# Values split into two float32r parts, tokens kept by super tile, and later weights turned earlier in a four-layer graph kernel

## The chip, the cores and the metric

The kernel runs on one core of one Trainium2 chip. A core has five engines that run their own instruction streams and wait for each other through semaphores: TensorE (PE; its weight loads are listed as PEld), VectorE (DVE), ScalarE (ACT), GpSimd (POOL) and SyncE (SP), which here does nothing but issue transfers. Transfers run on 16 DMA engines and are issued from SP, ACT or POOL. The metric is the device time of one execution in microseconds (us), as the median of several runs.

## The reference, cut to what matters

There are N = 3327 tokens x of 128 features, a dense matrix adj (3327 x 3327), and four layers, each followed by a residual and a layer norm. Layer 0 is an attention over 128 "slots" with 8 values each; the other three are graph layers with adj.

```python
# layer 0: n, d = x.shape; h = 8
q = (x @ Wq.T).reshape(d, n, h)
k = (x @ Wk.T).reshape(d, n, h)
v = (x @ Wv.T).reshape(d, n, h)
a = einsum('dnh,dmh->dnm', q, k) * scale + adj + adj
out = einsum('dnm,dmh->dnh', softmax(a, axis=2), v).reshape(n, h * d) @ Wo.T
x = layernorm(x + out)
# layers 1 to 3: adj (normalized) @ x, times small weights, residual, layernorm
```

The reshape is plain: the 3327 x 1024 result of a projection is read in memory order as 128 rows of 3327 x 8. So slot row d begins at token 3327 d / 128, mostly not at a multiple of anything convenient, and the q, k and v of one slot row come from about 26 neighbouring tokens.

## The kernel before, in words

The kernel has three stages. In the profiled execution the prologue lasts until the first exponential at 339 us, the attention until the last exponential starts at 10,018 us, and the three graph layers until the end at 10,791 us. The change touches the prologue alone (lines 243 to 408).

**The prologue** goes through the tokens in NU = 7 super tiles of 512 tokens (the last has 255). `load_by_h` loads and transposes Wq, Wk and Wv. For every super tile x is loaded (`xr`, line 264), transposed on TensorE (`xtr`, line 271) and copied to SBUF in two orders: `xT` by VectorE for q and k, and `xN` by ScalarE for the values. Before, all seven super tiles have room in one `xT` and one `xN`.

The main loop then takes each super tile u in turn.

- `split` (line 339) makes q, and then k: `products` (two matmuls of 512 columns a slot of 128 tokens) into a PSUM buffer `pp` of which there are two; ScalarE writes the rounded high part `hi` as float32r, VectorE the remainder `lo`, and VectorE reduces `hi` to a maximum (`top_q` or `top_k`, line 348). POOL issues the stores of `hi` and `lo` to DRAM (`q_s`, `k_s`), 2 MB each.
- `values_projected` (line 303) makes the values transposed, one matmul a head h into a PSUM buffer `pv`, copied by ScalarE and VectorE in turn to `vp`.
- `values_turned(d)` (line 312) brings the values of two slot rows d and d + 1 into the layout that the attention reads: a matmul with a shifted identity (a 128 column window of `turn`, which is zeros, identity, zeros) moves tokens to their partition and transposes at once. A slot row's window can lie across the end of the partitions (`wrap`) and two super tiles, so one call has some four matmuls, mostly of 8 x 26 = 208 columns, into a PSUM buffer `vtr`. VectorE and ScalarE copy these in turn to `vo`, and after every eight calls ScalarE issues four stores `v_img<-vo` (line 336).
- For u = 1 to 4 a row tile `ar` of adj is loaded by SP (line 88 in `load_rows`) and its maximum `tops` taken by VectorE (line 368). `ar` and `vo` share the tag "wide", of which there are two buffers. `store_tops` (line 217) writes the maxima in pieces of 4 bytes to `lead_s`.

`xtr`, `pv` and `vtr` share three PSUM buffers (tag "ps"); `w_ps`, for the transposes of weights, has one.

After the loop, in the order of the text, the weights of later layers (w1, w3, wo) are loaded, transposed and stored to DRAM, and a global maximum is reduced over partitions (`topall`, line 391) into a flag.

**What sets the order.** In the prologue a scheduler orders each engine's instructions by its own estimate of times; an engine then runs them strictly in that order. It moves work across the text: in the program as built, the transposes of x stand several super tiles ahead of their use, and those of w1, w3 and wo lie between matmuls from super tile 1 on. The attention has its order written out by hand (`manual_schedule`, line 663 on) and is the same before and after. Its SBUF pools take the room of the prologue's, so its first load (`e_in`, line 439) waits until all of the prologue's transfers are done.

Of the kernel before, what the change touches and what calls it, by code (L numbers as in the profile page):

```python
# [10 lines left out]
F32 = mybir.dt.float32  # L11
F32R = mybir.dt.float32r
I32 = mybir.dt.int32
AF = mybir.ActivationFunctionType
# [5 lines left out]
P = 128  # L20
# [30 lines left out]
def kernel(ctx: ExitStack, tc: tile.TileContext, x, adj, wq, wk, wv, wo,  # L51
# [193 lines left out]
    with tc.tile_pool(name="pw", bufs=1) as pw, tc.tile_pool(name="pa", bufs=2) as pa, \  # L245
# [9 lines left out]
        xT = pw.tile([P, NU, 4, P], F32, name="xT")  # L255
        xN = pw.tile([P, NU * SUPER], F32, name="xN")
        wqT = load_by_h(pw, ppw, wq, "wqT")
        for u in range(NU):
            base, R, full, rest = spread(u)
            xr = pa.tile([P, 4, D], F32, name="xr")  # L260
# [11 lines left out]
            nc.vector.tensor_copy(xT[:, u, 0:R, :], ps[:, 0:R, :])  # L272
            nc.scalar.copy(xN[:, base:base + R * P].rearrange("c (p r) -> c r p", r=R), ps[:, 0:R, :])
            if u == 0:
                wkT = load_by_h(pw, ppw, wk, "wkT")
                wvT = load_by_h(pw, ppw, wv, "wvT")
# [9 lines left out]
        def products(u, r, w):  # L286
            pp = pps.tile([P, HD], F32, tag="pp", name="pp")
            for c in range(0, HD, 512):
                nc.tensor.matmul(pp[:, c:c + 512], lhsT=xT[:, u, r, :], rhs=w[:, c:c + 512], start=True, stop=True)
            return pp.rearrange("p (h j) -> p h j", h=H)  # L290
# [7 lines left out]
        turn = pw.tile([P, 3 * P], F32, name="turn")  # L298
        nc.gpsimd.memset(turn, 0.0)
        nc.gpsimd.tensor_copy(turn[:, P:2 * P], ident)  # L300
        vp, vo = {}, {}

        def values_projected(u):
            n = spread(u)[1] * P
            vp[u] = pa.tile([P, H, SUPER], F32, name="vp")
            for h in range(H):
                ps = pps.tile([P, SUPER], F32, tag="ps", bufs=3, name="pv")
                nc.tensor.matmul(ps[:, 0:n], lhsT=wvT[:, h * D:(h + 1) * D], rhs=xN[:, u * SUPER:u * SUPER + n],
                                 start=True, stop=True)
                copy(h, vp[u][:, h, 0:n], ps[:, 0:n])  # L310

        def values_turned(d):
# [5 lines left out]
            for k in range(2):  # L318
                q, r = (d + k) * N // D, (d + k) * N % D
                for wrap in range(2 if r else 1):  # L320
                    at = q + wrap
                    while at < q + wrap + T:
# [4 lines left out]
                        nc.tensor.matmul(ps[:, k, :, s:s + n], lhsT=turn[:, first:first + P],  # L327
                                         rhs=vp[u][:, :, at - u * SUPER:at - u * SUPER + n],
                                         start=(k == 0 and wrap == 0 and s == 0), stop=True,
                                         skip_group_check=True)  # L330
# [26 lines left out]
        for u in range(NU):  # L357
            split(u, wqT, q_s, top_q, SCALE / 2)
# [6 lines left out]
            if 1 <= u <= 4:  # L365
                ar = pa.tile([P, NP], F32, tag="wide", name="ar")
                load_rows(nc.sync, ar[:, 0:N], adj, u - 1)
                nc.vector.tensor_reduce(tops[:, u - 1:u], ar[:, 0:N], AX.X, ALU.max)
            if u == 4:
                store_tops(pw, 0, tops, P)  # L370
        assert d == D

        w1T = load_transposed(pw, ppw, w1, "w1T")
        nc.gpsimd.dma_start(out=w1T_s, in_=w1T.rearrange("p a b -> p (a b)"))
        w3T = load_transposed(pw, ppw, w3, "w3T")
        nc.gpsimd.dma_start(out=w3T_s, in_=w3T.rearrange("p a b -> p (a b)"))

        wo_raw = pw.tile([P, HD], F32, tag="w_raw", name="wo_raw")
        nc.sync.dma_start(out=wo_raw, in_=wo)
        woT = pw.tile([P, HD], F32, name="woT")  # L380
        for h in range(H):
            ps = ppw.tile([P, P], F32, tag="w_ps", name="w_ps")
            nc.tensor.transpose(ps, wo_raw.rearrange("p (j h) -> p h j", h=H)[:, h, :], ident)
            copy(h, woT[:, h * D:(h + 1) * D], ps)
        nc.gpsimd.dma_start(out=woT_s, in_=woT)
# [863 lines left out]
```

## Time and profile before

| | |
|---|---|
| median of 3 runs | 10783.05 us (10782.16 to 10786.95) |
| profiled execution | 10792.99 us, span 10791.2 us |
| TensorE, VectorE, ScalarE busy over the span | 10545.2, 8700.0, 9680.6 us |
| last value store's copies end, first load of the attention, first exponential | 310.0, 317.1, 339.1 us |
| moved by DMA from 0 to 360 us | 86.51 MB |

Three kinds of answers are used below. A row of a group of instructions has: line, engine, operation, tile written <- tiles read, shapes, count | total busy us, mean ns of one | idle time of the engine just before, and what ended it. A row of windows has: stretch, length, then busy time (and count) of PE, PEld, DVE, ACT and POOL, granted TensorE clock, DMA share and GB/s. A row of the timeline has: start, length, engine, line, operation, count, and in brackets the idle time ahead of it with what ended it. A float32 matmul shows as two records; a float32r matmul or a transpose as one. [...]records in a stream overlap, and their spacing is what they cost.

### The profile page before, as it was taken

The numbers are of one execution on the slowest core, as the hardware profiler recorded it, in microseconds if no ns is written. First come the engines' busy times: TensorE is split into PE (matmuls) and PEld (weight loads), VectorE is DVE, ScalarE is ACT, GpSimd is POOL, SyncE is SP. The second block draws the span as 40 slices with busy tenths as digits, with TensorE's granted clock in tenths as the row PEclk, the third lists the DMA queues.
The fourth block names the chain that finished last, engine by engine and source line by source line (L and its number), as shares of the span: only waits on it lengthen the run. The fifth ranks groups of instructions, "written<-read, shape, count | busy, mean of one in ns | idle before, by whom it ended". The sixth has DMA issues, their size and how long they took to land. (4 is left out here: it accounts for less than half of the span.)

```text
span 10791.2 us, 203132 instructions
## 1 busy us (share of the span) xinstructions
PE 10545.2 (98%) x76941; PEld 4103.4 (38%) x76941; DVE 8700.0 (81%) x9695; ACT 9680.6 (90%) x10559; POOL 1852.8 (17%) x2742
## 2 busy tenths in 40 slices
PE   8899999999999999999999999999999999999999
PEld 5333333333333333333333333333333333333779
DVE  6688998889988899888899788998889877788412
ACT  3799999999999999999999999999999999999400
POOL 0111122111221122211122111121112100001200
PEclk9899999999999999999999999999999999999999
DMA  7888888888888888888888788888888888888676
GB/s 251 156 129 124 131 139 136 128 126 129 136 140 125 125 132 135 137 125 128 129 139 137 116 123 122 125 132 129 129 128 126 124 120 118 115 114 121 214 281 246
DMA packets 995965, 1516.25 MB, mean 141 GB/s; under 512 B 203368, under 2 KB 813474, under 8 KB 981164
## 3 DMA queue, kind: packets, MB, share of 16 engines
q1 hardware_dynamic: 897750, 1371.76, 78.7%
q0 software_dynamic: 79616, 116.88, 4.9%
q8 instruction: 624, 10.22, 0.5%
q10 hardware_dynamic: 17620, 14.49, 0.4%
q14 instruction: 355, 2.90, 0.1%
HBM read 1371.86 MB, written 130.35 MB: 139 GB/s over the span
## 5 line engine op out<-in xcount | busy, mean ns | idle before, releaser
L618 ACT ACTIVATE e<-sc 128x952 f32<-128x952 f32 (+1 forms) x10080 | 9458.5, 1090 | 247.6 <-PE sc L610 216.5
L636 PE MATMUL o<-e,v_pad 128*32 128x476 f32 (+1 forms) x46592 | 5621.3, 573 | 38.2 <-DVE acc L649 25.5
L610 PE MATMUL sc<-qt,kt 64*128 64x476 f32 x23296 | 4470.2, 438 | 113.8 <-ACT e L618 63.6
L610 PEld LDWEIGHTS sc<-qt,kt 64*128 64x128 f32 x23296 | 2166.0, 184 | 4415.6 <-ACT e L618 3840.0
L580 DVE SCALAR_TENSOR_TENSOR e<-e,ey 128x952 f32<-128x952 f32 x2016 | 2319.7, 1151 | 66.4
L515 POOL COPY v_pad<-vs 128x192 f32<-128x192 f32 (+1 forms) x896 | 606.7, 702 | 7666.8 <-DMA vs<-v_img 5875.9
L636 PEld LDWEIGHTS o<-e,v_pad 128*32 128x32 f32 (+1 forms) x46592 | 1045.1, 108 | 1967.2 <-issue 1931.9
L574 DVE TENSOR_SCALAR ey<-sc 128x952 int32<-128x952 f32 x672 | 772.1, 1149 | 624.6 <-PE sc L610 615.1
L501 DVE CAST qt<-qt 64x1904 fp32r<-64x1904 f32 x896 | 1041.5, 1162 | 30.4
L499 DVE TENSOR_SCALAR qt<-qt 32x1428 fp32r<-32x1428 f32 x896 | 809.0, 903 | 140.4 <-DMA qt<-q_s 109.5
L234 POOL DMA_DIRECT2D adjT_s<-at x1352 | 853.5, 638 | 232.6 <-DMA adjT_s<-at 168.2
L580 DVE SCALAR_TENSOR_TENSOR e<-ey 128x952 f32<-128x952 f32 x672 | 773.5, 1151 | 23.3
L580 DVE SCALAR_TENSOR_TENSOR e<-e,et 128x952 f32<-128x952 f32 x672 | 774.1, 1152 | 20.7
L1085 PE MATMUL bank<-y,eT 128*128 128x128 f32 (+1 forms) x4056 | 473.9, 276 | 0.4 <-DVE h L1207 0.4
L1085 PEld LDWEIGHTS bank<-y,eT 128*128 128x128 f32 (+1 forms) x4056 | 465.3, 192 | 5.7 <-DVE h L1207 0.6
L577 DVE TENSOR_SCALAR ey<-ey 128x952 int32<-128x952 int32 x672 | 447.1, 665 | 23.3
L575 DVE TENSOR_SCALAR et<-ey 128x952 int32<-128x952 int32 x672 | 443.1, 659 | 22.5
L500 DVE TENSOR_SCALAR qt<-qt 32x476 fp32r<-32x476 f32 x896 | 385.7, 430 | 6.2 <-DMA qt<-lead_s 3.2
L649 DVE TENSOR_TENSOR acc<-o,acc 128x476 f32<-128x476 f32 x231 | 150.4, 651 | 248.8 <-PE o L636 247.6
L1045 ACT ACTIVATE rstd<-mv,eps 128x1 f32<-128x1 f32 x104 | 30.4, 293 | 265.2 <-DVE mv L1043 265.2
L656 POOL DMA_DIRECT2D o_s<-acc x308 | 238.7, 779 | 30.0 <-DVE acc L649 20.2
L647 DVE COPY acc<-o 128x476 f32<-128x476 f32 x77 | 50.1, 650 | 136.4 <-PE o L636 135.8
(151 smaller groups left out, 2357.8 us busy)
## 6 DMA issues: line engine op xcount, KB each, us to landing
kt<-k_s SPq DMA_DIRECT2D x5320, 96.0 KB
kt<-k_s SPq DMA_DIRECT2D x1764, 128.0 KB
eT<-adjT_s SPq DMA_DIRECT2D x78, 1664.0 KB
qt<-q_s SPq DMA_DIRECT2D x896, 119.0 KB
qt<-q_s SPq DMA_DIRECT2D x1792, 59.5 KB
vs<-v_img SPq DMA_DIRECT2D x224, 224.0 KB
adjT_s<-at POOLq DMA_DIRECT2D x1352, 32.0 KB, 6.3
vs<-v_img SPq DMA_DIRECT2D x224, 192.0 KB
```

Of the source, the lines that this page charges most:

```text
L234: nc.gpsimd.dma_start(out=flat_ap(adjT_s, (t * P + 32 * q) * NP + c * PIECE, [[NP, 32], [P, ns], [1, P]]), in_=at[32 * i:32 * i + 32].rear ...
L499: return [(0.9, None, lambda: nc.vector.tensor_scalar(qt[32:64, 1:], qf[0:32, 0:GROUP - 1], -1.0, None, ALU.mult)), (0.4, None, lambda: nc ...
L501: (1.2, None, lambda: nc.vector.tensor_copy(qt[64:128], qf[0:64]))]
L515: nc.gpsimd.tensor_copy(vp[:, 32:32 + nt * GROUP * 32].rearrange("p (x c) -> p x c", c=32)[:, :, 0:H], vs.rearrange("p (x c) -> p x c", c=H))
L574: nc.vector.tensor_scalar(yi, x, -58 * math.log(2.0), 2 ** 24 / math.log(2.0), ALU.max, ALU.mult)
L575: vec.append((0.7, of, lambda: nc.vector.tensor_scalar(ti, yi, UPPER, EXPONENT, ALU.bitwise_and, ALU.bitwise_xor)))
L577: vec.append((0.7, of, lambda: nc.vector.tensor_scalar(yi, yi, LOWER, QUARTER, ALU.bitwise_and, ALU.bitwise_or)))
L580: vec.append((1.2, of, lambda i=i, a=a: nc.vector.scalar_tensor_tensor(e, e if i else y, a, t if i == len(POLY) - 1 else y, ALU.add, ALU.m ...
L610: nc.tensor.matmul(s[:, i, 0:CW], lhsT=kt[64 * rg:64 * rg + 64, k, pos * P:(pos + 1) * P], rhs=qt[64 * rg:64 * rg + 64, k, :], start=False ...
L618: nc.scalar.activation(e[:, 0:n, :], s[:, 0:n, 0:CW], AF.Exp, scale=2.0)
L636: nc.tensor.matmul(o[32 * j:32 * j + 32, 0:CW], lhsT=values[b, g][:m, c:c + 32], rhs=es[b, g * GROUP + j, r][:m, :], start=(r == 0 and u = ...
L1085: nc.tensor.matmul(ps[:n, 0:D], lhsT=e[:m, s, :n], rhs=y[:m, s, col:col + D], start=(s == 0), stop=(s == T - 1))
```

## The change

There are three parts.

1. The projected values are kept as two float32r parts: `hi`, written by ScalarE from PSUM with rounding, and `lo`, the remainder, by VectorE from PSUM and `hi`. `values_turned` multiplies each part with a shifted identity in float32r and sums both in PSUM. Where a window has an odd number of tokens, both parts go through a float32 matmul with a float32 identity (`moves`) instead.
2. `xT` and `xN` are tiles of one super tile in a pool of two, and `tokens_turned(u)` is called at the start of super tile u instead of for all u ahead of the loop. This makes room for the second part of `vp`.
3. The weights w1, w3 and wo are loaded, transposed and stored within the loop, after super tile 2, instead of after the loop.

```diff
--- before.py
+++ after.py
@@ -252,11 +252,13 @@
             R = (n + P - 1) // P
             return base, R, n // R, n % R
 
-        xT = pw.tile([P, NU, 4, P], F32, name="xT")
-        xN = pw.tile([P, NU * SUPER], F32, name="xN")
+        xTs, xNs = {}, {}
         wqT = load_by_h(pw, ppw, wq, "wqT")
-        for u in range(NU):
+
+        def tokens_turned(u):
             base, R, full, rest = spread(u)
+            xTs[u] = pa.tile([P, 4, P], F32, name="xT")
+            xNs[u] = pa.tile([P, SUPER], F32, name="xN")
             xr = pa.tile([P, 4, D], F32, name="xr")
             if rest:
                 nc.gpsimd.memset(xr[96:P], 0.0)
@@ -269,11 +271,12 @@
             ps = pps.tile([P, 4, P], F32, tag="ps", bufs=3, name="xtr")
             for r in range(R):
                 nc.tensor.transpose(ps[:, r, :], xr[:, r, :], ident)
-            nc.vector.tensor_copy(xT[:, u, 0:R, :], ps[:, 0:R, :])
-            nc.scalar.copy(xN[:, base:base + R * P].rearrange("c (p r) -> c r p", r=R), ps[:, 0:R, :])
-            if u == 0:
-                wkT = load_by_h(pw, ppw, wk, "wkT")
-                wvT = load_by_h(pw, ppw, wv, "wvT")
+            nc.vector.tensor_copy(xTs[u][:, 0:R, :], ps[:, 0:R, :])
+            nc.scalar.copy(xNs[u][:, 0:R * P].rearrange("c (p r) -> c r p", r=R), ps[:, 0:R, :])
+
+        tokens_turned(0)
+        wkT = load_by_h(pw, ppw, wk, "wkT")
+        wvT = load_by_h(pw, ppw, wv, "wvT")
 
         def store_slots(eng, dram, row, u, sb):
 
@@ -286,7 +289,7 @@
         def products(u, r, w):
             pp = pps.tile([P, HD], F32, tag="pp", name="pp")
             for c in range(0, HD, 512):
-                nc.tensor.matmul(pp[:, c:c + 512], lhsT=xT[:, u, r, :], rhs=w[:, c:c + 512], start=True, stop=True)
+                nc.tensor.matmul(pp[:, c:c + 512], lhsT=xTs[u][:, r, :], rhs=w[:, c:c + 512], start=True, stop=True)
             return pp.rearrange("p (h j) -> p h j", h=H)
 
         top_q = pw.tile([P, NU], F32, name="top_q")
@@ -295,19 +298,24 @@
 
 
 
-        turn = pw.tile([P, 3 * P], F32, name="turn")
-        nc.gpsimd.memset(turn, 0.0)
-        nc.gpsimd.tensor_copy(turn[:, P:2 * P], ident)
+        moves = pw.tile([P, 3 * P], F32, name="moves")
+        nc.gpsimd.memset(moves, 0.0)
+        nc.gpsimd.tensor_copy(moves[:, P:2 * P], ident)
+        turn = pw.tile([P, 3 * P], F32R, name="turn")
+        nc.gpsimd.tensor_copy(turn, moves)
         vp, vo = {}, {}
 
         def values_projected(u):
             n = spread(u)[1] * P
-            vp[u] = pa.tile([P, H, SUPER], F32, name="vp")
+
+            vp[u] = [pa.tile([P, H, SUPER], F32R, name=f"vp{i}") for i in range(2)]
             for h in range(H):
                 ps = pps.tile([P, SUPER], F32, tag="ps", bufs=3, name="pv")
-                nc.tensor.matmul(ps[:, 0:n], lhsT=wvT[:, h * D:(h + 1) * D], rhs=xN[:, u * SUPER:u * SUPER + n],
+                nc.tensor.matmul(ps[:, 0:n], lhsT=wvT[:, h * D:(h + 1) * D], rhs=xNs[u][:, 0:n],
                                  start=True, stop=True)
-                copy(h, vp[u][:, h, 0:n], ps[:, 0:n])
+                hi, lo = vp[u][0][:, h, 0:n], vp[u][1][:, h, 0:n]
+                nc.scalar.activation(hi, ps[:, 0:n], AF.Copy)
+                nc.vector.scalar_tensor_tensor(lo, ps[:, 0:n], 1.0, hi.bitcast(F32), ALU.mult, ALU.subtract)
 
         def values_turned(d):
 
@@ -324,10 +332,13 @@
                         n = min(q + wrap + T, (u + 1) * SUPER) - at
                         s = at - q - wrap
                         first = (0 if wrap else P) + r
-                        nc.tensor.matmul(ps[:, k, :, s:s + n], lhsT=turn[:, first:first + P],
-                                         rhs=vp[u][:, :, at - u * SUPER:at - u * SUPER + n],
-                                         start=(k == 0 and wrap == 0 and s == 0), stop=True,
-                                         skip_group_check=True)
+                        for part in range(2):
+                            shift, parts = turn[:, first:first + P], vp[u][part][:, :, at - u * SUPER:at - u * SUPER + n]
+                            if n % 2:
+                                shift, parts = moves[:, first:first + P], parts.bitcast(F32)
+                            nc.tensor.matmul(ps[:, k, :, s:s + n], lhsT=shift, rhs=parts,
+                                             start=(k == 0 and wrap == 0 and s == 0 and part == 0), stop=True,
+                                             skip_group_check=True)
                         at += n
             copy(d // 2, vo[g][:, i // 4, :, i % 4 * H:(i % 4 + 2) * H].rearrange("p s (k h) -> p k h s", k=2), ps)
             if i == 14:
@@ -355,6 +366,8 @@
 
         d = 0
         for u in range(NU):
+            if u:
+                tokens_turned(u)
             split(u, wqT, q_s, top_q, SCALE / 2)
             split(u, wkT, k_s, top_k, 1.0)
             values_projected(u)
@@ -366,23 +379,24 @@
                 ar = pa.tile([P, NP], F32, tag="wide", name="ar")
                 load_rows(nc.sync, ar[:, 0:N], adj, u - 1)
                 nc.vector.tensor_reduce(tops[:, u - 1:u], ar[:, 0:N], AX.X, ALU.max)
+            if u == 2:
+
+                w1T = load_transposed(pw, ppw, w1, "w1T")
+                nc.gpsimd.dma_start(out=w1T_s, in_=w1T.rearrange("p a b -> p (a b)"))
+                w3T = load_transposed(pw, ppw, w3, "w3T")
+                nc.gpsimd.dma_start(out=w3T_s, in_=w3T.rearrange("p a b -> p (a b)"))
+
+                wo_raw = pw.tile([P, HD], F32, tag="w_raw", name="wo_raw")
+                nc.sync.dma_start(out=wo_raw, in_=wo)
+                woT = pw.tile([P, HD], F32, name="woT")
+                for h in range(H):
+                    ps = ppw.tile([P, P], F32, tag="w_ps", name="w_ps")
+                    nc.tensor.transpose(ps, wo_raw.rearrange("p (j h) -> p h j", h=H)[:, h, :], ident)
+                    copy(h, woT[:, h * D:(h + 1) * D], ps)
+                nc.gpsimd.dma_start(out=woT_s, in_=woT)
             if u == 4:
                 store_tops(pw, 0, tops, P)
         assert d == D
-
-        w1T = load_transposed(pw, ppw, w1, "w1T")
-        nc.gpsimd.dma_start(out=w1T_s, in_=w1T.rearrange("p a b -> p (a b)"))
-        w3T = load_transposed(pw, ppw, w3, "w3T")
-        nc.gpsimd.dma_start(out=w3T_s, in_=w3T.rearrange("p a b -> p (a b)"))
-
-        wo_raw = pw.tile([P, HD], F32, tag="w_raw", name="wo_raw")
-        nc.sync.dma_start(out=wo_raw, in_=wo)
-        woT = pw.tile([P, HD], F32, name="woT")
-        for h in range(H):
-            ps = ppw.tile([P, P], F32, tag="w_ps", name="w_ps")
-            nc.tensor.transpose(ps, wo_raw.rearrange("p (j h) -> p h j", h=H)[:, h, :], ident)
-            copy(h, woT[:, h * D:(h + 1) * D], ps)
-        nc.gpsimd.dma_start(out=woT_s, in_=woT)
 
         top = pw.tile([P, 2], F32, name="top")
         nc.vector.tensor_reduce(top[:, 0:1], top_q, AX.X, ALU.max)
```

In the program as built the following also differs: each super tile's transposes of x come after the `vtr` matmuls of the one before; the last four of a super tile's value remainders stand on VectorE behind the maximum `top_k`; `tops` of the second and third `ar` stand amid the `vo` copies of super tiles 2 and 3; SP has the loads of the later weights ahead of the first `ar` and a load of x behind each; and POOL has the store of wo between the k stores of super tile 2 and the q stores of super tile 3. Four loads for the attention's first background piece (`ai`), which SP issued in the first 10 us, are now at their place in the attention.

## The prediction

> **What bounds the kernel now.** I read the page first: ScalarE is 90% busy and TensorE 98%, nearly all of it in the attention, which the change leaves alone. So the change is worth what it does to the prologue, and I cut the trace there at the first projected-value matmul (`vtr`) of each super tile (windows view: busy time of PE, PEld, DVE, ACT, POOL, then clock, DMA share, GB/s).
>
> ```profile
> 84.80:126.30 41.50, 38.01 (x134) 23.91 (x133) 28.49 (x21) 14.44 (x18) 4.11 (x5) 0.96 0.79 287
> 126.30:168.40 42.10, 37.74 (x134) 24.05 (x133) 28.48 (x22) 14.63 (x18) 3.54 (x4) 0.96 0.82 293
> 168.40:213.40 45.00, 39.30 (x135) 24.82 (x134) 28.56 (x22) 14.48 (x18) 4.11 (x5) 0.92 0.73 265
> 213.40:251.90 38.50, 33.69 (x125) 23.78 (x123) 17.55 (x16) 12.25 (x17) 2.65 (x3) 0.91 0.73 257
> ```
>
> A super tile takes some 42 us; TensorE works 38 of them, VectorE 28.5, ScalarE 14.5. TensorE leads, VectorE is not far behind. The prologue's groups give the unit prices:
>
> ```profile
> L327 PE MATMUL vtr<-vp,turn 128*128 128x208 f32 x486 | 95.1, 355 | 6.0 <-ACT vo L141 5.9
> ...
> L346 DVE SCALAR_TENSOR_TENSOR lo<-pp,hi 128x1024 fp32r<-128x1024 f32 x52 | 62.7, 1220 | 34.1 <-ACT hi L345 34.1
> ...
> L348 DVE TENSOR_REDUCE top_q<-hi 128x1 f32<-128x4096 f32 x6 | 26.5, 4409 | 0.0
> ...
> L143 DVE COPY vp<-pv 128x512 f32<-128x512 f32 x24 | 15.6, 684 | 8.5 <-PE pv L308 8.4
> ...
> L141 ACT COPY vp<-pv 128x512 f32<-128x512 f32 x24 | 14.0, 584 | 12.0 <-PE pv L308 12.0
> ```
>
> The timelines of super tiles 2 and 3, taken engine by engine (start and length in us, engine, line; in brackets the idle time before it), show the wait that I think decides:
>
> ```profile
> 134.89 4.64 ACTq L336 DMA_DIRECT2D v_img<-vo  x4
> ...
> 145.62 0.33 SPq L88 DMA_DIRECT2D ar<-in_adj_dram  x1
> ...
> 152.63 3.62 DVE L368 TENSOR_REDUCE tops<-ar 128x1 f32<-128x3327 f32 x1 [5.34 <-DMA ar<-in_adj_dram]
> ...
> 157.44 5.40 PE L289 MATMUL pp<-wkT,xT 128*128 128x512 f32 x8 [4.14 <-DVE lo L346]
> ...
> 168.42 12.10 PE L327 MATMUL vtr<-vp,turn 128*128 128x208 f32 x68
> ```
>
> `ar`, a row tile of adj, shares two buffers with `vo`: its load starts only when a value store has landed (10.7 us after that store's issue), and its maximum 7.0 us later, 17.7 in all. The other three such chains take, likewise, 14.9 (96.26 to 111.12), 19.9 and 14.6. VectorE stands still for it, and 4 us later TensorE stands.
>
> **What the Trainium skill says.** (1) "TensorE: Matmul & The Clock Gate", the table at its head and Part 1: ScalarE and VectorE are strict FIFOs. The trace agrees: `lo` waits behind `tops` for 5.34 + 3.6 us. (2) The same page, Part 1: an idle window of some 3.4 us puts the array at half clock. The trace agrees: after the 4.14 us gap eight records took 5.40, elsewhere 3.60 us. (3) "FP8 and Floating Point Precision", TensorE Precision Notes: true FP32 is four passes, the reduced reading one. The trace agrees at 476 columns only (below). (4) "DMA: Bandwidth & Descriptors", Anatomy of one DMA: semaphore waits happen on the issuing sequencer; so SP's `ar` blocks what follows it there.
>
> **The change, part by part.** *Matmuls with shifted identities.* 267 float32 matmuls go; each is two records at (12.10 - 0.36)/67 = 0.175 us, so 0.35 us, together 93. In their place 534: 510 float32r, and 24 with an odd column count stay float32. The trace has float32r at 476 columns alone (the scores), shortest record 368 ns. Float32 records of 128, 208 and 512 columns take 276, 355 and 600 ns, that is 170 ns plus about 0.84 a column; 368 is 170 plus 0.42 a column, and one record, not two. At 208 columns this makes 87 ns; the skill's weight-load price (same TensorE page, LDWEIGHTS) is 128/1.2 = 107 if it isn't hidden. I take 0.10. The upper bound, if few columns lose the single pass, is 0.35 each. At 0.10 TensorE gains 93 - 53 = 40 us; at 0.35 it loses 94.
>
> *Value evictions.* 28 VectorE and 28 ScalarE copies become 56 ScalarE copies and 56 VectorE subtractions that wait for them. A subtraction of 512 costs no more than the 684 ns copy (1220 for 1024). VectorE gains 48 x 0.69 + 8 x 0.42 - 18 = 18 us of work, ScalarE 15, which hides in its idle two thirds (15 us if it didn't). VectorE's is not hidden. From the built order, super tile 1 and later: VectorE does `xT`, two `lo`, one value part, two `lo`, the 4.41 us maximum, two `lo`, three value parts, two `lo`, the other maximum, the last four value parts; only then can `vtr` start. Before, the second maximum ran beside `vtr`. Walk, from the last `vtr` of the tile before: xr's transposes and the copies ahead 1.1, `xT` 0.7, product 1.9, `hi` 1.0, so the first `lo` starts at 4.9; then 8 x 1.14 + 2 x 4.33 + 8 x 0.61 (spacings when back to back) = 22.7, and 3.6 us of gaps in which `lo` waits for `hi` or the last value part for its PSUM buffer: `vtr` at 31.2. TensorE idles 4.9 us of that before the last value product, goes cold, and that product and the first `vtr` lose 0.9 + 1.3. `vtr` takes 84 x 0.10 = 8.4. A tile without `ar` costs 31.2 + 0.9 + 1.3 + 8.4 = 41.8 us, against 38.5 to 45: the TensorE gain is used up.
>
> *Tokens by super tile.* x's transposes (0.5 us of TensorE a tile) ran well ahead of use and now come after each tile's `vtr`; their `xT` copy is behind all older VectorE work. The loads of x on SP stand behind `ar`, but one tile ahead of use: nothing. Two `ar` maxima are now placed amid `vtr`, ahead of the next `xT`. The chain takes at least 14.6; I use 14.8. Tile 2: its store is issued after five `vo` copies, 5 x 0.84 + 1.3 + 1.1 + 0.3 = 6.9 after `vtr` starts, the maximum starts at 21.7, ends 25.3, `vo` and `xT` follow to 26.9; without it `xT` ends at 11.5: +15.4. Tile 3: store at 5.1, `xT` at 25.9: +14.4. The first maximum, now ahead of tile 2's second `lo`: store 7 x 0.84 + 2.7 = 8.6 after tile 1's `vtr` starts, maximum 14.8 later; it is wanted 9.7 + 6.1 = 15.8 after that start and so waits 7.6; with its own 3.6, less 2.0 of gaps that it fills, +9.2. Tile 5's lands in time: +3.6.
>
> *Weights turned earlier.* The scheduler had already spread these (w1's at 78.7 us, half of wo's from 207), so little moves: 11 transposes and copies, three loads on SP, now all ahead of the first `ar`, three stores on POOL, woT's amid the q and k stores instead of last. They fall into TensorE's gaps; uncovered, 11 x (0.27 + 0.29) = 6 us. POOL's partition reduce no longer waits behind woT's store (313.7); the first queries, held by the flag until 321.45, go 2.6 us sooner. `turn`'s float32r copy on POOL ends 50 us before use; the four early `ai` loads move to where they are needed, steps later: nothing.
>
> *Sum.* First `vtr` 54 (as before), tile 0's 70 matmuls to 61; tile 1, 41.8 more, to 102.8; tile 2's `vtr` 32.1 + 9.2 later at 144.1, the next `xT` 26.9 on at 171.0; tile 3's `vtr` 30.3 after that at 201.3, `xT` 227.2; tile 4's `vtr` 257.5, to 267.2; tile 5's 302.9, to 312.6; tile 6, with half the tokens, 20 + some 3 in which `lead_s`, stored in 4-byte pieces, clogs the queues (273 to 280 us before, 20 GB/s), `vtr` 5: 341. Before: 309 (308.95). Less 2.6: +29 us. The profiled execution has 10793.0 us (span 10791.2), 10 above the median of 10783; on the median this makes **10812 us**.
>
> **Rivals.**
> 1. *Few columns keep float32r slow* (0.35 us). TensorE then loses 94 us, tiles 2 and 3 hide some 20 of their part behind the chain of `ar`; 17 + 21 + 10 + 7 + 21 + 21 + 10 - 6 = 101 (tile by tile, less 6 of the first wait) more than above: 10913. For it: no such form in the trace. Against: one pass at 476 columns. Halfway (0.17) would be near 10835.
> 2. *The chain of `ar` is short.* The change clears the queue of q and k stores before the value store, so store and load could land in 9 instead of 14.8, and the clock may stay up: 29 - 2 x 6 - 7 - 6 = +4: 10787, no change that a measurement can tell (0.2%, 21.6 us, is about what it can). Against: the two least crowded chains took 14.6 and 14.9.
> 3. *Faster*: TensorE sets the pace and VectorE keeps up. 40 us of matmul gain, 2.6 at the end, less some 5 of turnaround: 10745. It decides if the value parts run beside `vtr` rather than ahead; the built order, and 24 us of VectorE work before each `vtr`, are against it.
> 4. *It does nothing*, as 97% of the span is the attention and the later layers: holds if the prologue's end stays within 20 us, counted in 2.
>
> **Chances.** Main case 0.43, rival 1 0.28 (with halfway), rivals 2 and 4 0.22, rival 3 0.07. The likeliest case alone: 10805 to 10835. Range 10776 to 10922: below it lie most of rival 3, above it a part of rival 1. Slower than 0.2%: 0.71, within 0.22, faster 0.07.
>
> **What would show it.** Right: `vtr` records spaced 0.09 to 0.11; `tops` waiting some 10 us for `ar` twice, TensorE idle there at half clock, the first exponential near 368 instead of 339; the attention's length unchanged. Wrong: `vtr` spaced 0.17 or more (rival 1), waits for `ar` under 4 us (rival 2), super tiles of 35 us (rival 3), or an attention that itself changes.

## The result and the profile after

The changed kernel takes 10830.9 us (median of five runs, 10830.5 to 10835.1) against 10785.2 for the kernel before (10782.2 to 10787.4), run beside it: a ratio of 1.0044, with a 95% interval of 1.0032 to 1.0055. That is 45.7 us, or 0.4%, slower. The forecast was slower, 10812, with a likeliest range of 10805 to 10835.

The cut of the trace at the first `vtr` of each super tile, as for the kernel before (windows view: busy time of PE, PEld, DVE, ACT, POOL, then TensorE's clock, DMA share, GB/s):

```profile
58.13:97.04 38.91, 30.86 (x125) 17.50 (x126) 28.17 (x26) 16.38 (x20) 4.67 (x6) 0.99 0.62 220
97.04:142.57 45.53, 35.95 (x147) 21.70 (x145) 26.39 (x27) 17.75 (x24) 1.78 (x2) 0.90 0.62 221
142.57:206.70 64.13, 39.16 (x146) 23.52 (x144) 37.74 (x29) 18.78 (x25) 5.89 (x7) 0.80 0.65 236
206.70:266.24 59.54, 40.20 (x142) 24.66 (x141) 31.48 (x26) 17.86 (x22) 4.06 (x5) 0.79 0.57 206
266.24:318.96 52.72, 38.58 (x142) 23.84 (x141) 31.81 (x27) 17.97 (x22) 5.07 (x6) 0.82 0.72 255
```

None is shorter than before. In the kernel before the first stretch, from 54.02 to 84.80, took 30.8 us; here it is 38.9, at full clock, with TensorE busy for 30.9. The third and fourth are 64 and 60 us long, where the kernel before had 45 and less. No engine is busy for more than 68% of them, and the clock is at 0.8: they are stretches of waiting. The prologue's groups (each with busy time and mean of one, then the idle time just before and what ended it) name the waits:

```profile
L339 PE MATMUL vtr<-vp,turn 128*128 128x208 f32 x486 | 67.6, 303 | 7.0 <-DVE vp L318 3.8 <-ACT vo L141 2.5 <-issue 0.6
...
L292 PE MATMUL pp<-wqT,xT 128*128 128x512 f32 x104 | 56.4, 685 | 34.9 <-DVE xT L274 27.7 <-DVE lo L357 6.9 <-ACT wqT L141 0.4
...
L318 DVE SCALAR_TENSOR_TENSOR vp<-pv,vp 128x512 fp32r<-128x512 f32 x48 | 30.9, 683 | 9.6 <-ACT vp L317 9.6
...
L381 DVE TENSOR_REDUCE tops<-ar 128x1 f32<-128x3327 f32 x4 | 14.5, 3619 | 30.1 <-DMA ar<-in_adj_dram 30.1
```

TensorE's `vtr` fell from 95.1 to 67.6 us of busy time (there are 486 records of 208 columns in both kernels: two parts of one record each stand where one product of two records stood). But the four maxima of `ar` now wait 30.1 us (10.7 before), and TensorE waits 27.7 us for the next `xT`. VectorE's timeline of super tile 2 (start and length in us, in brackets the idle time before) has the forecast order, though only two remainders stand behind the maximum here and not four:

```profile
143.65 4.41 DVE L359 TENSOR_REDUCE top_k<-hi 128x1 f32<-128x4096 f32 x1
147.97 1.28 DVE L318 SCALAR_TENSOR_TENSOR vp<-pv,vp 128x512 fp32r<-128x512 f32 x2
...
158.79 0.90 DVE L143 COPY vo<-vtr 128x416 f32<-128x416 f32 x1 [0.90 <-PE vtr L339]
170.94 3.62 DVE L381 TENSOR_REDUCE tops<-ar 128x1 f32<-128x3327 f32 x1 [11.24 <-DMA ar<-in_adj_dram]
174.47 0.84 DVE L143 COPY vo<-vtr 128x416 f32<-128x416 f32 x1
175.16 0.67 DVE L274 COPY xT<-xtr 128x512 f32<-128x512 f32 x1
```

First the remainders of the values stand behind the 4.41 us maximum; then the maximum of `ar` waits 11.2 us amid the copies `vo`, and `xT` is behind it. TensorE's timeline shows what follows:

```profile
58.81 7.86 PE L339 MATMUL vtr<-vp,turn 128*128 128x208 f32 x68 [0.23 <-DVE vp L318]
...
175.89 6.53 PE L292 MATMUL pp<-wqT,xT 128*128 128x512 f32 x8 [12.99 <-DVE xT L274]
...
235.38 5.81 PE L292 MATMUL pp<-wqT,xT 128*128 128x512 f32 x8 [11.73 <-DVE xT L274]
...
281.64 3.70 PE L292 MATMUL pp<-wqT,xT 128*128 128x512 f32 x8 [1.08 <-DVE xT L274]
```

It stands 13.0 and 11.7 us, and the eight records after these gaps take 6.5 and 5.8 us, where eight take 3.7 after a short gap.

The first exponential is at 383.9 us, 44.8 later than the 339.1 of before: the whole loss is in the prologue. From there to the last exponential the two profiled executions differ by 6 us the other way (the last exponential ends at 10057.9 in the changed kernel, at 10019.6 before), which is no more than executions of one kernel differ by: those of before spread over 13 us beside runs 1 to 4 below. From the first exponential to the end, all fourteen profiled executions of this document take between 10444.5 and 10456.3 us (10452.1 before, 10444.8 in the changed kernel). So nothing shows that the attention itself has changed, and a difference of less than some 12 us between two single executions says little.

### The profile page after: what moved, and what is told of

It reads as the page before. It is cut to its first block, busy times and chain, and to the rows that moved or that the text cites. A ratio compares the mean times of both kernels' runs of the same rounds, so it can differ in the third digit from the quotient of the medians.

```text
span 10828.7 us, 203219 instructions
## 1 busy us (share of the span) xinstructions
PE 10536.4 (97%) x76965; PEld 4084.1 (38%) x76965; DVE 8722.5 (81%) x9723; ACT 9697.7 (90%) x10587; POOL 1850.7 (17%) x2743
## 5 line engine op out<-in xcount | busy, mean ns | idle before, releaser
L589 DVE TENSOR_SCALAR et<-ey 128x952 int32<-128x952 int32 x672 | 444.0, 661 | 22.4
## 6 DMA issues: line engine op xcount, KB each, us to landing
qt<-q_s SPq DMA_DIRECT2D x1792, 59.5 KB
```

The lines of the kernel that those rows point to most:

```text
L589: vec.append((0.7, of, lambda: nc.vector.tensor_scalar(ti, yi, UPPER, EXPONENT, ALU.bitwise_and, ALU.bitwise_xor)))
```

## The experiments

Theory 1 is that of the prediction: TensorE's gain is used up because VectorE's value remainders stand behind `top_k`, and the chain value store, load of `ar`, maximum, now amid `vtr`, does the rest. The rivals are that the tokens kept by super tile are the loss in themselves, that TensorE (cold, or with slow float32r) sets the pace, and that the chain is hidden. Each run was timed beside the kernel before:

| kernel | us | ratio to before, 95% interval |
|---|---|---|
| changed | 10830.9 | 1.0044 (1.0032 to 1.0055) |
| 1 `ar` in its own buffer | 10802.9 | 1.0014 (1.0007 to 1.0020) |
| 2 values first | 10824.9 | 1.0033 (1.0021 to 1.0046) |
| 3 tokens and weights alone | 10797.7 | 1.0010 (1.0002 to 1.0019) |
| 4 weights alone | 10788.1 | 1.0001 (0.9993 to 1.0010) |
| 5 as 1, short maxima | 10773.7 | 0.9987 (0.9980 to 0.9994) |
| 6 before, short maxima | 10775.4 | 0.9989 (0.9982 to 0.9996) |
| 7 as 1, values first | 10788.7 | 1.0001 (0.9992 to 1.0010) |
| 8 as 7, maxima in pieces | 10790.5 | 1.0003 (0.9994 to 1.0012) |
| 9 all shifts in float32 | 10910.1 | 1.0112 (1.0097 to 1.0128) |
| 10 as 7, value stores on SyncE | 10781.2 | 0.9995 (0.9986 to 1.0003) |
| 11 as 10, keys' maximum later | 10760.6 | 0.9976 (0.9965 to 0.9986) |
| 12 before, value stores on SyncE | 10779.2 | 0.9992 (0.9983 to 1.0000) |

The median of before was 10785.2 beside the changed kernel and lay between 10786.5 and 10787.3 beside the runs, so that a difference between two rows carries 1 to 2 us from that alone.

### 1: the chain of `ar` taken away

```diff
-            xr = pa.tile([P, 4, D], F32, name="xr")
+            xr = pa.tile([P, 4, D], F32, name="xr", bufs=1)
...
-                ar = pa.tile([P, NP], F32, tag="wide", name="ar")
+                ar = pa.tile([P, NP], F32, tag="ar", name="ar", bufs=1)
```

> The changed kernel, with the adj rows `ar` in a buffer of their own instead of the pair that they share with `vo` (x's rows `xr` keep one buffer instead of two, to make room). The load of `ar` then waits for no value store, and the built order has all four maxima in super tile 0, none amid `vtr`. Theory 1 (the chain value store, `ar` load, maximum is what costs the time): the waits of 5.6, 11.2, 10.8 and 2.5 us and two of the maxima amid `vtr` go, some 35 us; super tile 0 pays back 5 to 15 for four loads of 1.7 MB and four maxima of 3.6 us. So 20 to 35 us below the changed kernel: 10796 to 10811. Rival (the value remainders on VectorE and the cold TensorE alone set the length of a super tile, the chain is hidden by them): within 8 us of the changed kernel.

10802.9, 28 us below the changed kernel and inside the expectation. The windows from the first `vtr` of super tile 1 to that of super tile 5:

```profile
107.30:150.33 43.03, 34.68 (x145) 21.37 (x144) 28.60 (x27) 18.25 (x24) 4.09 (x5) 0.94 0.67 240
150.33:195.57 45.24, 36.44 (x143) 21.56 (x141) 28.29 (x25) 17.90 (x22) 3.55 (x4) 0.88 0.65 238
195.57:243.31 47.74, 38.92 (x142) 24.63 (x141) 28.30 (x25) 17.87 (x22) 3.54 (x4) 0.86 0.62 227
243.31:286.63 43.32, 33.78 (x141) 19.99 (x140) 28.13 (x24) 17.79 (x22) 4.06 (x5) 0.97 0.77 273
```

Against the 45.5, 64.1, 59.5 and 52.7 of the changed kernel these four give back 42.6 us. Super tile 0 pays 9.2 (its first `vtr` at 67.3 instead of 58.1, with the four loads and maxima in it), so 33 remain, and TensorE's first matmul of the attention (`sc<-ident,e_in`) is 33.0 us sooner, at 333.22 instead of 366.19. The chain, with the maxima's own time in the super tiles, was worth some 30 us; the rival falls. What stays are super tiles of 43 to 48 us, no shorter than those of the kernel before.

### 2: the values first

```diff
             split(u, wqT, q_s, top_q, SCALE / 2)
-            split(u, wkT, k_s, top_k, 1.0)
             values_projected(u)
+            split(u, wkT, k_s, top_k, 1.0)
```

> The changed kernel, with the values projected ahead of the keys' split, so that VectorE does all remainders of the values before the keys' maximum of 4.41 us and `vtr` may start beside that maximum. The two maxima of `ar` stay amid `vtr` in super tiles 2 and 3. Theory 1 (the value remainders that stand behind the 4.41 us maximum set the start of `vtr`): up to 4 us a super tile, less what the three PSUM buffers of `vtr` give back, since the VectorE copies `vo` still stand behind that maximum: 2 to 3.5 us in each of six, 12 to 20 us below the changed kernel, 10811 to 10819. Rival (TensorE or the chain of `ar` sets the pace everywhere): within 6 us of it.

10824.9: 6 us where 12 to 20 were expected (8, if each is set against the kernel before beside it). Theory 1's expectation is missed, and the time is at the rival's bound. The first `vtr` of super tile 0 came at 51.2 instead of 58.1, as it should; but the gain went into a new wait. TensorE's timeline of super tile 1 in this run, and the group of `vtr`:

```profile
92.70 3.36 PE L339 MATMUL vtr<-vp,turn 128*128 128x144 f32 x28
99.22 7.25 PE L339 MATMUL vtr<-vp,turn 128*128 128x208 f32 x48 [3.16 <-DVE vo L143]
```

```profile
L339 PE MATMUL vtr<-vp,turn 128*128 128x208 f32 x486 | 79.3, 332 | 25.5 <-DVE vo L143 19.5 <-ACT vo L141 5.7 <-DVE vp L318 0.2
```

`vtr` starts beside the keys' maximum, fills its three PSUM buffers and stands for VectorE's `vo`, which is behind that same maximum: 19.5 us in all. The chain takes a part, too: the maxima of `ar` wait 35.8 us here instead of 30.1. The remainders' place does set the start of `vtr`, but to move them alone mostly moves the wait, from `vp` to `vo` and to `ar`.

### 3 and 4: tokens and weights, without the values in two parts

Run 3 is the changed kernel with the values as before:

```diff
-            vp[u] = [pa.tile([P, H, SUPER], F32R, name=f"vp{i}") for i in range(2)]
+            vp[u] = pa.tile([P, H, SUPER], F32, name="vp")
...
-                hi, lo = vp[u][0][:, h, 0:n], vp[u][1][:, h, 0:n]
-                nc.scalar.activation(hi, ps[:, 0:n], AF.Copy)
-                nc.vector.scalar_tensor_tensor(lo, ps[:, 0:n], 1.0, hi.bitcast(F32), ALU.mult, ALU.subtract)
+                copy(h, vp[u][:, h, 0:n], ps[:, 0:n])
```

> Tokens by super tile and the later weights amid the prologue as in the changed kernel, but the values in float32 in one part, copied and turned as before. The built order has no maximum of `ar` amid `vtr`: each stands after the next super tile's `xT` and one or two value copies, nearly as before. Theory 1 (the value remainders on VectorE and the chain that they push amid `vtr` are what costs): near the kernel before, with 1 to 2 us more a super tile for the late `xT` and 3 less at the end: 10783 to 10800. Rival (keeping tokens by super tile is itself the loss, through the wait for `xT` and the cold TensorE after it): 10820 or more.

Run 4 is the kernel before with the part `if u == 2:` of the change and no other line of it.

> The kernel before, with the later layers' weights turned in super tile 2 and nothing else changed. Both theories: little moves, some 3 us sooner at the end and up to 6 us for transposes that find no gap: within 0.1% of before, 10776 to 10792.

Both as expected: 10797.7 and 10788.1, that is 11 and 1 us above before. In run 3 the four maxima of `ar` wait 12.5 us, not 30, and none stands amid `vtr`. So some 10 us of the 46 (the interval of run 3 reaches from 2 to 20) go to the tokens by super tile, nothing measurable to the weights, and the other 35 came with the values in two parts, which the tokens by super tile make room for: through VectorE's work, and through the order in which the scheduler then put the maxima of `ar`. The values in two parts without the tokens by super tile weren't tried: SBUF has no room for them then.

### 5 and 6: is it VectorE?

```diff
-            nc.vector.tensor_reduce(top[:, u:u + 1], hi[:, :, 0:R, :].bitcast(F32), AX.XYZ, ALU.max,
+            nc.vector.tensor_reduce(top[:, u:u + 1], hi[:, 0, 0:R, :].bitcast(F32), AX.XY, ALU.max,
                                     apply_absolute_value=True)
```

> The run with `ar` in its own buffer, and each maximum `top_q` and `top_k` taken over one head of eight instead of all eight; the maxima over the other seven heads are left out. Each maximum then takes some 0.6 us instead of 4.41, and nothing else is taken from VectorE. Theory 1 (VectorE's chain of remainders and maxima sets a super tile's length once `ar` is out of the way): 6 to 7.6 us in each of six whole super tiles until TensorE's 33 us show, 30 to 45 us below that run: 10758 to 10773, and the waits of the last value product for VectorE (4.7 us, three times) gone. Rival (TensorE, cold after each turnaround, or the copies `vo` set it): less than 12 us below it, 10791 or more.

> The kernel before with the same short maxima over one head of eight (the maxima over the other seven heads are left out). The built order moves the first maximum of `ar` a super tile's few instructions as well. Theory 1 (there TensorE sets the pace and the maxima run beside it): at most 10 us below before, 10773 to 10787. Rival (VectorE set the pace of the kernel before, too): 25 us or more below it, 10760 or less.

The same edit, which leaves out work and is no version to keep, gives 29 us in run 5 (below run 1) and 12 in run 6 (below before). Theory 1 asked for 30 to 45 and for at most 10: both miss it by 1 to 2 us, and both are far from the rivals (less than 12; 25 or more). VectorE's maxima are worth more than twice as much after the change as before it. The groups of value products in runs 1 and 5, and that of `vtr` in run 5, show where the time came from and what comes next:

```profile
L314 PE MATMUL pv<-xN,wvT 128*128 128x512 f32 x96 | 53.3, 672 | 22.4 <-DVE vp L318 22.4
...
L314 PE MATMUL pv<-xN,wvT 128*128 128x512 f32 x96 | 50.0, 636 | 6.0 <-DVE vp L318 6.0
...
L339 PE MATMUL vtr<-vp,turn 128*128 128x208 f32 x486 | 64.9, 296 | 14.4 <-ACT vo L141 13.6 <-issue 0.6
```

The value products' wait for VectorE falls from 22.4 to 6.0 us, and TensorE now stands 13.6 us for ScalarE's copies `vo` (4.8 in run 1).

### 7 and 8: order and pieces

Run 7 joins the edits of 1 and 2. Run 8 has in addition, in place of the one maximum, four in the loop over `r`:

```diff
+                nc.vector.tensor_reduce(top[:, 4 * u + r:4 * u + r + 1], hi[:, :, r, :].bitcast(F32), AX.XY, ALU.max,
+                                        apply_absolute_value=True)
```

> `ar` in its own buffer, and the values projected ahead of the keys' split. With the values first alone the gain was 6 us, since TensorE then stood 3 us a super tile for the VectorE copies `vo`, which wait behind the keys' maximum. Theory 1 (the work of VectorE as a whole, whatever its order, sets the super tile): 0 to 12 us below the run with `ar` in its own buffer alone, 10791 to 10803. Rival (only the order of the remainders and the maximum counts, hidden in that run by the chain of `ar`): 20 us or more below it, 10783 or less.

> As the last, and the maxima `top_q` and `top_k` taken in four pieces of 1024 elements, one after each remainder `lo`, each into its own column (x's turned copy `xN` keeps one buffer to make room). Nothing is left out. Theory 1 (VectorE's waits of 1 to 2 us for `hi` can take in a piece of 1.1 us, so that no copy or remainder stands behind 4.41 us): 3 to 6 us in each of six super tiles below the last, 10760 to 10785, at or below the kernel before. Rival (TensorE's wait for each `lo` then grows by the piece ahead of it): no better than the last.

Run 7 took 10788.7, 14 us below run 1 and level with the kernel before: a little more than theory 1 allowed, less than the rival asked. With the chain out of the way, the edit of run 2 is worth about twice what it was there. Run 8 missed its expectation: 10790.5 is no better than run 7, as the rival said, but hardly by the rival's mechanism, since TensorE's waits for `lo` grew from 2.4 to 4.3 us only. A wait that is longer than that is in run 7 already, in TensorE's group of `vtr` and in ScalarE's timeline (the group of four value stores stands on ScalarE's own queue):

```profile
L339 PE MATMUL vtr<-vp,turn 128*128 128x208 f32 x486 | 77.3, 326 | 28.6 <-DVE vo L143 19.0 <-ACT vo L141 8.2 <-ACT vp L317 0.7
...
225.89 0.93 ACT L141 COPY vo<-vtr 128x416 f32<-128x416 f32 x1 [0.31 <-PE vtr L339]
226.85 8.68 ACTq L347 DMA_DIRECT2D v_img<-vo  x4
235.71 1.58 ACT L141 COPY vo<-vtr 128x416 f32<-128x416 f32 x2 [8.88 <-issue]
```

VectorE's last copy of `vo` before the store, behind `top_k` there, ended at 232.7; the group of stores ended 2.8 us after that (it takes 3.1 where nothing is late), and ScalarE's next two copies stood behind it. In run 8 one such group took 8.84 us, and TensorE waited 17.2 us for ScalarE's `vo` in all, 9 more than in run 7.

### 9: the price of `vtr`

```diff
-                            if n % 2:
-                                shift, parts = moves[:, first:first + P], parts.bitcast(F32)
+                            shift, parts = moves[:, first:first + P], parts.bitcast(F32)
```

> The changed kernel with every product with a shifted identity in float32 (both parts are kept, the order of the work too), so that only TensorE's price of a `vtr` changes. 510 of them take 0.35 us instead of the 0.113 measured: 121 us more of TensorE. Theory 1 (`vtr` stands in a row with VectorE's remainders and is hidden only where TensorE waits for the chain of `ar`, some 10 us in each of super tiles 2 and 3): 90 to 115 us above the changed kernel, 10920 to 10945. Rival (TensorE has so much slack after the change that VectorE alone sets the length): less than 60 above, 10890 or less.

10910.1, 79 us above the changed kernel, between the two, so that neither is right. Of some 121 us more of TensorE, a third is hidden. The maxima of `ar` show where: they wait 10.3 us in place of 30.1, since the longer `vtr` covers the loads (this view ends at 420 us and has 902 of the 972 records of `vtr`):

```profile
L338 PE MATMUL vtr<-vp,moves 128*128 128x208 f32 x902 | 168.5, 347 | 3.2 <-DVE vp L318 2.6 <-issue 0.6
...
L380 DVE TENSOR_REDUCE tops<-ar 128x1 f32<-128x3327 f32 x4 | 14.5, 3616 | 10.3 <-DMA ar<-in_adj_dram 10.3
```

On TensorE's side, the waits ahead of its four groups of products (q, k, the values and `vtr`) fell from 74.9 to 43.7 us, and the records of the first three took 6 us less: 37 of the 42 us that are hidden. TensorE isn't free in the changed kernel: two thirds of what `vtr` costs is on the path, so it stands in a row with VectorE's work more than beside it.

### 10, 11 and 12: from there to a faster kernel

```diff
-                    nc.scalar.dma_start(out=flat_ap(v_img, k0 * HD + g * 4 * w, [[T * HD, P], [w, 4], [1, w]]),
+                    nc.sync.dma_start(out=flat_ap(v_img, k0 * HD + g * 4 * w, [[T * HD, P], [w, 4], [1, w]]),
```

> The run with `ar` in its own buffer and the values first, and the stores of `vo` issued by SyncE instead of ScalarE. In that run ScalarE stands up to 8.7 us in one group of these stores, waiting for VectorE's last copy, and its own copies `vo` behind it hold up TensorE for 8.2 us in all. Theory 1 (the stores' wait on ScalarE's queue is a wait that the shorter super tile exposes): 6 to 14 us below that run, 10774 to 10783, a little below the kernel before. Rival (the two buffers of `vo` are waited for anyway, until their stores have landed): within 4 us of that run.

10781.2, some 7 us below run 7, as expected, though the two intervals overlap. TensorE's 8.2 us of waiting for ScalarE's `vo` are gone, and the 19.0 for VectorE's are left:

```profile
L339 PE MATMUL vtr<-vp,turn 128*128 128x208 f32 x486 | 76.5, 325 | 20.5 <-DVE vo L143 19.0 <-ACT vp L317 0.7 <-DVE vp L318 0.6
```

The same line in the kernel before is run 12:

> The kernel before with the stores of `vo` issued by SyncE instead of ScalarE. There TensorE waits for ScalarE's copies `vo` 5.9 us in all. Theory 1 (this wait belongs to the shorter super tiles and is small here; the loads of `ar` on SyncE stand behind the stores that they wait for anyway): 0 to 6 us below before, 10780 to 10787. Rival (the issue of the stores on ScalarE is a cost of the kernel before as much as of the changed one): 8 us or more below it.

It took 8.1 us off: more than theory 1 allowed, and what the rival asked, though the interval (0.9983 to 1.0000) holds both answers. The trace of before speaks for the rival. Two groups of value stores held ScalarE for long there, and TensorE stood behind both:

```profile
217.05 9.50 ACTq L336 DMA_DIRECT2D v_img<-vo  x4
227.71 8.57 PE L327 MATMUL vtr<-vp,turn 128*128 128x208 f32 x32 [4.39 <-ACT vo L141]
...
272.16 13.70 ACTq L336 DMA_DIRECT2D v_img<-vo  x4
288.21 1.22 PE L308 MATMUL pv<-xN,wvT 128*128 128x256 f32 x2 [9.24 <-ACT vp L141]
```

In the changed kernel no group took more than 3.6 us. So the wait on ScalarE's queue is not peculiar to the change; it was there before, and came back in runs 7 and 8.

Run 11 takes the 19 us. `split` leaves the keys' maximum out and hands `hi` back; the loop does it one super tile later:

```diff
             if u:
                 tokens_turned(u)
+                nc.gpsimd.tensor_copy(top_k[:, u - 1:u], xTs[u][:, 0, 0:1])
+                largest(u - 1, hi_k, top_k)
```

> The run with the value stores on SyncE, and each keys' maximum `top_k` held back until the next super tile's `xT` is copied (a copy of one column on GpSimd into its place, before it is written, holds it). The built order then has it between `xT` and the first `lo`, where VectorE waits 3 to 5 us for `hi`, and no longer ahead of the copies `vo`. Nothing is left out. Theory 1 (the 4.41 us maximum ahead of VectorE's `vo` is what TensorE waits for, 19 us in six super tiles): 12 to 20 us below that run, 10761 to 10770, below the kernel before by more than a measurement's uncertainty. Rival (VectorE's sum of work sets the length, wherever the maximum stands): within 6 us of that run.

10760.6: 21 us below run 10, a little more than expected, and 0.24% below the kernel before (0.14 to 0.35%). Of the versions that leave nothing out it is the fastest, and the only one with its whole interval clear of the kernel before. TensorE's wait for VectorE's `vo` is gone (19.0 us in run 10). VectorE's timeline has the maximum where it costs TensorE little, between `xT` and the first `lo`; TensorE's waits for `lo` grew from 0.7 to 2.3 us in all:

```profile
171.81 0.85 DVE L143 COPY vo<-vtr 128x416 f32<-128x416 f32 x1 [0.88 <-PE vtr L339]
172.52 0.67 DVE L274 COPY xT<-xtr 128x512 f32<-128x512 f32 x1
173.46 4.42 DVE L351 TENSOR_REDUCE top_k<-hi 128x1 f32<-128x4096 f32 x1 [0.28 <-POOL top_k L376]
177.80 2.35 DVE L361 SCALAR_TENSOR_TENSOR lo<-pp,hi 128x1024 fp32r<-128x1024 f32 x2
```

and the windows from the first `vtr` of super tile 1 to that of super tile 5 show TensorE leading at full clock in three of four:

```profile
88.54:122.95 34.41, 32.28 (x145) 19.95 (x144) 28.37 (x27) 18.62 (x24) 4.30 (x6) 1.00 0.95 360
122.95:157.47 34.52, 32.58 (x148) 20.13 (x146) 28.37 (x28) 19.14 (x26) 4.30 (x6) 1.00 0.88 315
157.47:192.06 34.59, 32.26 (x142) 19.76 (x141) 28.25 (x25) 18.70 (x23) 3.72 (x5) 1.00 0.85 305
192.06:240.21 48.15, 34.35 (x141) 20.45 (x140) 28.02 (x25) 18.30 (x22) 4.25 (x6) 0.86 0.70 248
```

These three take 34 to 35 us, where the changed kernel has 46 to 64. The fourth has the next bound in it:

```profile
217.65 0.85 DVE L143 COPY vo<-vtr 128x416 f32<-128x416 f32 x1 [12.18 <-DMA v_img<-vo]
```

A value store isn't done when its buffer is wanted again, and VectorE, then TensorE, stand 12 us. The DMA queues were 85 to 95% busy in the three stretches before; that this is what held up the store is likely, but no run tests it.

What run 11 doesn't show is how much of its 27 us below before belongs to float32r. The stores on SyncE alone gave the kernel before 8 us (run 12), and shortened maxima 12 (run 6). If these add up, the kernel before would stand near 10767 (an estimate from these two runs), and the kernel before with all the edits of run 11 wasn't tried. What is shown is that the three stretches of 34 to 35 us are shorter than the 38 to 39 us of TensorE's work alone in those of the kernel before.

## Why the prediction was right, and where its sum was short

**The order on VectorE (right).** The remainders do stand behind `top_k`. TensorE waits 4.72 us for the last value product in super tiles 3, 4 and 5 (4.9 forecast), and the two records of that product then take 2.08 us, twice the 1.02 of two records elsewhere:

```profile
256.92 2.74 PE L314 MATMUL pv<-xN,wvT 128*128 128x512 f32 x6
264.38 2.08 PE L314 MATMUL pv<-xN,wvT 128*128 128x512 f32 x2 [4.72 <-DVE vp L318]
```

From the end of `vtr` in super tile 0 (66.5) to that in super tile 1 (108.6) are 42.1 us; 41.8 were worked out. In run 1, where no super tile from 1 on has an `ar` in it, the same stretch takes 41.6 to 48.7 us, 44.4 on average, so the walk fits the shortest and is otherwise 1.5 to 7 us short. Runs 5 and 11 show that much of the lost time comes back when the maximum is out of the way, 29 and 21 us; run 2, that to move the remainders alone doesn't bring it back.

**The chain of `ar` (right; its sum came out better than its parts).** From the issue of the value store to the maximum it takes 14.2, 13.9 and 13.9 us in the first three (107.08 to 121.30, 157.04 to 170.94, 215.81 to 229.74); 14.8 was taken. The forecast adds 9.2, 15.4, 14.4 and 3.6 us in super tiles 2, 2, 3 and 5, 42.6 together. Run 1 against the changed kernel gives 42.6 over the same four windows, but as 2.5, 18.9, 11.8 and 9.4, so that so close an agreement is luck in part. The first two belong together: in super tile 2 ten records of `vtr` ran ahead of the wait for the last remainder, and the windows are cut at the first of them. Together they are 21.4 where 24.6 were forecast. Super tile 5 has 9.4 instead of 3.6, since its `ar` did not land in time. There the maximum waited 2.49 us, and with `top_q` behind it held TensorE for 7.93, so that eight cold records took 5.48.

**The price of `vtr` (right).** 68 records at full clock in 7.86 us, one matmul each, make (7.86 - 0.3)/67 = 0.113 us; 0.10 was taken, with 0.35 as the bound. It is nearer to the 107 ns that the prediction names for a weight load that isn't hidden than to its 87; no run tells the two apart. So float32r stays one record at 208 columns, at a third of float32's price. Rival 1 falls by this, and run 9 shows what it would have cost: 79 us, where the prediction had 101 above its main case. That its 10913 lies so near to run 9's 10910 is luck: the main case was 19 us too low, the addition 22 too high. One thing was priced wrongly: the 24 products with an odd count stay float32, but the sum took them at 0.10 as well. In super tile 5 four of them, as eight records, took 1.7 us.

**The terms that were too small.** At TensorE's first matmul of the attention (366.19 instead of 321.10) the loss is 45.1 us, not 29. The step that failed is the one that took super tile 0 as before ("first `vtr` 54 (as before)"): the remainders stand behind the maximum there, too, and its `vtr` ended at 66.5 instead of 61, +5.5 (its start 4.1 late, the rest the price). The `vtr` of super tile 4 took 13.7 instead of 9.7 and that of super tile 5 11.2 (each up to the next transposes of x): 0.113 for 0.10, the odd counts, and waits for `vo` that the sum did not have, +5.5 together. Super tile 5 before its `vtr` took 39.0 instead of 35.7, +3.3. Super tiles 2 and 3, beyond what they inherited, added 2.3, super tile 1 0.3 and the start of super tile 4 0.6. Super tile 6 took 24.8 instead of 28.4, -3.6: the 3 us for `lead_s` did not come. That sums to +14, and 2 more are from the end: TensorE goes on 0.8 us sooner after the last `vtr` than before, not 2.6. It waits 11.2 us there for the first rows `e_in` of adj, and their load is issued at 362.67, the moment at which VectorE's wait for the last value store (7.85 us) ends, not with the flag (363.73).

**The rivals.** The chain of `ar` was not short (rival 2). TensorE did not set the pace (rival 3); run 11 shows three super tiles as that rival described them, but stays at 10760.6 where it had 10745, and with other edits in it that help the kernel before as well. That the change does nothing (rival 4) falls with the prologue's end, 44.8 us later where that rival allowed 20.

## What to carry to other kernels

A faster operation on the leading engine gains only if the work that feeds and empties it keeps up. Before splitting operands in two to save TensorE's passes, add the remainders to the queue of the engine that must make them, and look at what long instruction stands ahead of them there. A long reduction whose result is wanted much later belongs into a wait that its engine has anyway; in this kernel its place alone was worth 21 us. And when a buffer is shared between a store and a load, its wait moves with every change of order: here the wait at a pair of shared buffers came to 30 us in one order and 11 in another.

## What the runs showed of the hardware

- An idle TensorE came back slow, and more so after longer gaps, if not evenly: eight records took 3.70 us after 1.1 us of idling, 5.48 after 7.9, 5.81 after 11.7 and 6.53 after 13.0. Four records after 5.4 us took 3.78 instead of 1.94, all of them at half speed. That half speed follows an idle window of some 3.4 us is what the Trainium skill says ("TensorE: Matmul & The Clock Gate", Part 1); the trace agrees, as the slow ones listed here all follow gaps longer than that and the quick one a gap of 1.1 us.
- A maximum on VectorE took 677, 1209 and 4409 ns for 512, 1024 and 4096 elements: 144 ns, and 1.04 ns an element, so that four pieces cost 0.43 us more than one whole. The Trainium skill ("VectorE: DVE Perf Modes", perf-mode tier table) gives this reduction the slowest mode alone; the measured slope, the same at all three sizes, fits that.
- Issuing a store isn't free for the engine that issues it: a group of four held ScalarE for 3.1 us at best, and for 8.7 when a part of its source was late (run 7), and the copies behind it as well. In the kernel before one group held ScalarE for 13.7 us, although the last copy into its source had ended at least 11 us before the group did; the cause of that is open.
